# An edge-attention loop on one core: loads three steps ahead, edge terms before sums on TensorE, a weight matrix moved in halves

## The chip, the cores and the metric

The kernel runs on one core of a Trainium2 chip. The metric is the device time of one launch in microseconds (us). The engines that matter are TensorE (PE: matmuls; PEld is its loading of weights), VectorE (DVE), ScalarE (ACT), GpSimd (POOL) and SyncE (SP, which here only issues transfers). Each runs its own list of instructions in order, and they wait for one another through semaphores. A transfer (DMA) is issued from the queue of an engine and lands on its own.

## The reference

Four layers follow each other, each a graph network (gnn), a mixing step over all nodes (mix) and a feed-forward step (ffn), on 3,125 nodes of 256 features and 103,125 directed edges sorted by target. The change lies in layer 3's gnn:

```
feat_src = (feat @ W_n).reshape(N, 8, 32)
el = einsum('nhd,hdt->nht', feat_src, attn_l)     # t: 4 kinds of edge
er = einsum('nhd,hdt->nht', feat_src, attn_r)
em = einsum('ef,hft->eht', edge_attr_16, attn_m)
e  = einsum('eht,et->eh', el[src] + er[dst] + em, edge_attr_4) / 3.0
e  = where(e > 0, e, 0.2 * e)
a  = segment_softmax(e, dst)
rst = segment_sum(feat_src[src] * a[:, :, None], dst)

x = x + L3_gnn(layernorm(x)) + L3_mix(layernorm(x))
x = x + L3_ffn(layernorm(x))
```

(The three einsums over t are written as one here.) em is called the edge terms below. The kernel computes exp(e) unnormalised, sums exp(e) * z and exp(e) per target, and divides at the end.

## The kernel before, in words

The sorted edges lie in 806 columns of 128, one edge on each partition. `edge_attention` takes them in 101 steps of SC = 8 columns. The targets are cut into 25 tiles of 125 nodes; a step touches one or two of them (`here[i]`). Before the loop a table in device memory is written that holds for each source node its 8 x 33 values (32 features and a 1 for each head) and its 32 attention terms.

The parts of a step i, with engine and line:

- `load(i)`, SP: the targets of the step's 1,024 edges, copied to 125 partitions (`row`, two transfers through `part_dma`, L584 and L585, 4 buffers), the edge features (`ef`, L2584, 4 buffers) and a mask (`mask`, L2586, 5 buffers).
- `gather(i)`, POOL: eight indirect transfers (L2592), one for each column, bring the table's rows of the sources into `z_edge` (3 buffers).
- `targets(i)`, DVE: `hot` (L2605, 3 buffers) is 1 where an edge's target is node n of the tile.
- `products(i)`, PE: four matmuls of the edge features (L2617), and those of `hot` with the target terms `er` (L2620), both into the one buffer of `p_m`. ACT copies it to `m_sb` (L2622).
- `turn(i)`, PE: two transposes of `m_sb` into `p_e` (L2627), which puts an edge's terms on its own partition.
- `weights(i)`: DVE adds the source's terms and multiplies by the mask (`l`, L2635, L2638), sums and applies the leaky slope (`e`, L2640, L2641). ACT takes the exponential (`near_e`, L2643). DVE builds `oh`, the edges' one-hot targets (L2647), and multiplies `z_edge` by `near_e` (L2651).
- `sums(i)`, PE: for each column a matmul of `oh` with `z_edge` into the tile's accumulator `p_acc` (L2660, 2 buffers).
- `divide(i)`, DVE: where a tile is complete, the division and the addition to x (L2668 to L2672). After some tiles, work of the feed-forward step on them becomes available.

Between these, `piece()` is called twice a step. It advances other work by one yield: first layer 3's mixing step (`mix3`), then the transfers of the last weight matrix (`part3`, L2833, five transfers of 1 MB from SP, used only after the loop by the routed feed-forward step), and then the feed-forward's first half (`hidden3`).

The loop is written in a software pipeline. Turn i of it issues, in this order: `load(i+2)`, `sums(i-2)`, `gather(i+1)`, `products(i)`, `weights(i-1)`, a piece, `targets(i+1)`, `divide(i-2)`, `turn(i)`, a piece. PE and DVE keep exactly this order (`manual_schedule`). On ACT, POOL and SP a planner places the instructions by estimated times, so a change of the written order can change their order too.

Of the kernel before, what the change touches and what calls it, by code (L numbers as in the profile page):

```python
# [22 lines left out]
P = 128  # L23
# [3 lines left out]
C = 256  # L27
# [32 lines left out]
def dview(ap, offset, dims):  # L60
    return bass.AP(tensor=ap.tensor, offset=ap.offset + offset, ap=[list(d) for d in dims])
# [1560 lines left out]
class Dense(Net):  # L1622
# [903 lines left out]
    def edge_attention(self, x, xT, weights, pieces, then):  # L2526
# [10 lines left out]
        with ExitStack() as s:  # L2537
            with ExitStack() as s2:
# [4 lines left out]
                for t in range(NT):  # L2543
                    p = ps.tile([TP, C + 2 * EC], F32, name="p_z")
# [22 lines left out]
            def piece():  # L2567
                while work:
                    try:
                        return next(work[0])  # L2570
                    except StopIteration:
                        work.pop(0)
# [6 lines left out]
            def load(i):  # L2579
                c0, n = steps[i]  # L2580
                rows[i] = w.tile([TP, SC * P], I16, name="row", bufs=4)
                self.part_dma(nc.sync, rows[i], dview(dst_d, c0 * P, [[0, TP], [1, SC * P]]))
                efs[i] = w.tile([P, 2 * P], F32, name="ef", bufs=4)
                nc.sync.dma_start(efs[i], ins["edge16_s"][i])  # L2584
                masks[i] = w.tile([P, SC, 4], F32, name="mask", bufs=5)
                nc.sync.dma_start(masks[i][:, :n, :], ins["edge4_t"][:, c0:c0 + n, :])  # L2586

            def gather(i):
                c0, n = steps[i]
                zs[i] = wz.tile([P, SC, W], F32, name="z_edge")  # L2590
                for j in range(n):
                    nc.gpsimd.indirect_dma_start(  # L2592
                        out=zs[i][:, j, :], out_offset=None, in_=table,
                        in_offset=bass.IndirectOffsetOnAxis(ap=src[:, c0 + j:c0 + j + 1], axis=0))

            def strips(i, t):
                c0, n = steps[i]
                return max(cols[t][0] - c0, 0) // 2, min(-(-(cols[t][1] - c0) // 2), 4)

            def targets(i):  # L2600

                for t in here[i]:
                    q0, q1 = strips(i, t)
                    hots[i, t] = w.tile([TP, SC * P], F32, name="hot", bufs=3)
                    nc.vector.tensor_tensor(hots[i, t][:, q0 * 256:q1 * 256], rows[i][:, q0 * 256:q1 * 256],  # L2605
                                            node[:, t:t + 1].to_broadcast([TP, (q1 - q0) * 256]), OP.is_equal)

            def products(i):

                p_m = ps.tile([P, 2 * P], F32, name="p_m")  # L2610
                for t in [None] + here[i]:
                    for q in range(4):
                        qs = slice(q * 256, (q + 1) * 256)
                        s = slice(32 * q, 32 * q + 32)
                        last = ([None] + [u for u in here[i] if strips(i, u)[0] <= q < strips(i, u)[1]])[-1]
                        if t is None:
                            nc.tensor.matmul(p_m[s, :], attn_m[32 * q:32 * q + 16, :], efs[i][32 * q:32 * q + 16, :],  # L2617
                                             start=True, stop=(last is None))
                        elif strips(i, t)[0] <= q < strips(i, t)[1]:
                            nc.tensor.matmul(p_m[s, :], er[:, t, :], hots[i, t][:, qs], start=False, stop=(t == last))  # L2620
                terms[i] = w.tile([P, 2 * P], F32, name="m_sb")
                nc.scalar.activation(terms[i], p_m, AF.Copy)  # L2622

            def turn(i):
                p_e = ps.tile([P, 2, P], F32, name="p_e")
                for j in range(2):
                    nc.tensor.transpose(p_e[:, j, :], terms[i][:, j * P:(j + 1) * P], self.ident)  # L2627
                terms[i] = p_e

            def weights(i):  # L2630

                c0, n = steps[i]
                z = zs[i]
                l = w.tile([P, SC // 2, 2, EC], F32, name="l", bufs=1)
                nc.vector.tensor_add(l[:, :n // 2], terms[i].rearrange("p j (q f) -> p q j f", f=EC)[:, :n // 2],  # L2635
                                     z[:, :n, HW:].rearrange("p (q j) f -> p q j f", j=2))
                l4 = l.rearrange("p q j (t h) -> p (q j) t h", h=H)[:, :n]
                nc.vector.tensor_mul(l4, l4, masks[i][:, :n, :, None].to_broadcast([P, n, 4, H]))  # L2638
                e = w.tile([P, SC, H], F32, name="e")[:, :n, :]
                nc.vector.tensor_reduce(e, l4.rearrange("p c t h -> p c h t"), AX.X, OP.add)  # L2640
                nc.vector.scalar_tensor_tensor(e, e, 0.2, e, op0=OP.mult, op1=OP.max)  # L2641
                weight = near_e[:, i % 4, :n, :]
                nc.scalar.activation(weight, e, AF.Exp, scale=1.0 / 3.0)  # L2643
                for t in here[i]:
                    a, b = max(cols[t][0], c0), min(cols[t][1], c0 + n)
                    ohs[i, t] = w.tile([P, SC, TP], F32, name="oh", bufs=4)
                    nc.vector.scalar_tensor_tensor(ohs[i, t][:, :b - a, :], iota[:, None, :].to_broadcast([P, b - a, TP]),  # L2647
                                                   float(t * TP), dst[:, a:b][:, :, None].to_broadcast([P, b - a, TP]),
                                                   op0=OP.add, op1=OP.is_equal)
                zh = z[:, :n, :HW].rearrange("p c (h d) -> p c h d", h=H)  # L2650
                nc.vector.tensor_mul(zh, zh, weight[:, :, :, None].to_broadcast([P, n, H, D + 1]))  # L2651

            def sums(i):
                c0, n = steps[i]
                for t in here[i]:
                    a, b = max(cols[t][0], c0), min(cols[t][1], c0 + n)
                    if a == cols[t][0]:
                        acc[t] = ps3.tile([TP, HW], F32, name="p_acc")
                    for k in range(a, b):
                        nc.tensor.matmul(acc[t], ohs[i, t][:, k - a, :], zs[i][:, k - c0, :HW], start=(k == cols[t][0]), stop=(k == cols[t][1] - 1))  # L2660
# [16 lines left out]

            last = len(steps)
            with tc.manual_schedule(engines={mybir.EngineType.PE, mybir.EngineType.DVE}):
                for i in range(2):  # L2680
                    load(i)
                gather(0)
                targets(0)
                for i in range(last + 2):
                    if i + 2 < last:
                        load(i + 2)
                    if i >= 2:
                        sums(i - 2)
                    if i + 1 < last:
                        gather(i + 1)  # L2690
                    if i < last:
                        products(i)
                    if 1 <= i <= last:
                        weights(i - 1)
                    piece()
                    if i + 1 < last:
                        targets(i + 1)
                    if i >= 2:
                        divide(i - 2)
                    if i < last:  # L2700
                        turn(i)
                    piece()
                while work:
                    piece()
# [123 lines left out]
        turned = b[:, 2 * Q + 3 * C:2 * Q + 3 * C + KC * 3 * TP].rearrange("p (k n) -> p k n", k=KC)  # L2828
        return parts, norm, turned

    def part3(self, queue, out, f):

        queue.dma_start(out.rearrange("p (e c) -> p e c", c=C), self.ins["L3_ffn_Wd"][:, f * P:(f + 1) * P, :].rearrange("e p c -> p e c"))  # L2833

    def pieces3(self, w, ps, x, xn, xT, mix, parts):

        yield from self.mix3(w, ps, x, xn, xT, mix)
        for f, o in enumerate(parts):
            self.part3(self.nc.sync, o, f)
            yield  # L2840
            yield

    def hidden3(self, w, ps, x, room, t0, nt, weights, ones, hid_d):

# [557 lines left out]
```

## Time and profile before

| what | value |
|---|---|
| time, median of 3 runs | 5431.47 us (5419.27 to 5449.77) |
| the profiled execution | 5439.84 us |
| its span | 5438.0 us, 74,923 instructions |
| its mean granted TensorE clock | 0.924 |
| busy over the span | PE 87%, PEld 53%, DVE 62%, ACT 31%, POOL 28% |
| edge loop of layer 3 | about 3930 to 5230 us |
| clock granted in 3930 to 4430, 4430 to 5230 | 0.81, 0.86 |
| L2660 in the loop | 556.8 us of PE, 2,032 records, median 386 ns of one |
| L2651 in the loop | 236.5 us of DVE, 101, 2,342 ns each |
| L2592 | 769.7 us of POOL, 806, 955 ns each |
| table loads for L2643 on ACT | 35 of 1,283 ns |

The profile of one execution lists each instruction with its start and its duration. A line of the timeline gives the start in us from the span's start, the duration, engine, line, operation, output <- inputs, shapes, how many were joined, and in brackets how long the engine had been idle and what ended that. "issue" stands for a wait in which nothing was outstanding that the profile shows, "remote" for a releaser that the profile could not name. PE's matmuls are pipelined, so rows of PE overlap a little, and rows show when a matmul ran, not when another engine learned of it.

### The profile page before, as it was taken

The numbers are of one execution on the slowest core, as the hardware profiler recorded it, in microseconds if no ns is written. First come the engines' busy times: TensorE is split into PE (matmuls) and PEld (weight loads), VectorE is DVE, ScalarE is ACT, GpSimd is POOL, SyncE is SP. The second block draws the span as 40 slices with busy tenths as digits, with TensorE's granted clock in tenths as the row PEclk, the third lists the DMA queues.
The fourth block names the chain that finished last, engine by engine and source line by source line (L and its number), as shares of the span: only waits on it lengthen the run. The fifth ranks groups of instructions, "written<-read, shape, count | busy, mean of one in ns | idle before, by whom it ended". The sixth has DMA issues, their size and how long they took to land.

```text
span 5438.0 us, 74923 instructions
## 1 busy us (share of the span) xinstructions
PE 4737.5 (87%) x28141; PEld 2874.3 (53%) x28141; DVE 3392.9 (62%) x5768; ACT 1669.0 (31%) x2863; POOL 1514.4 (28%) x1413
## 2 busy tenths in 40 slices
PE   6789999889898999999989999999767767777778
PEld 4554434468465443785554335556445544444557
DVE  6878888755447988553359993223366655565643
ACT  2569878611431111102320103333211012222221
POOL 1108857534100000000010000000266555555623
PEclk8899999889999999999999999999888888888879
DMA  3885545511201111110001112000255545444535
GB/s 89 78 74 157 163 124 150 163 59 62 70 3 30 37 41 31 41 40 5 15 24 37 35 28 65 7 1 1 79 136 141 143 140 146 127 136 142 152 116 173
DMA packets 351061, 443.50 MB, mean 82 GB/s; under 512 B 144972, under 2 KB 270175, under 8 KB 350248
## 3 DMA queue, kind: packets, MB, share of 16 engines
q1 hardware_dynamic: 266710, 222.80, 17.8%
q0 software_dynamic: 55024, 175.53, 11.4%
q10 hardware_dynamic: 28959, 40.29, 2.4%
q8 instruction: 228, 3.74, 0.3%
q14 instruction: 140, 1.15, 0.1%
HBM read 384.87 MB, written 56.78 MB: 81 GB/s over the span
## 4 chain that ended last, share of the span: by engine, by line
PE 69%; DVE 9%; issue 6%; another core or an unknown queue 5%; ACT 4%; DMA 4%; POOL 2%; ACTq 0%; SPq 0%; DVEq 0%; POOLq 0%
PE acc L2316 9%; PE p_tr L751 8%; PE p_acc L2660 7%; PE p_n L2156 5%; PE acc L2448 5%; PE acc L2321 4%; PE p_h L751 4%; PE p_y L751 4%; PE p_q L751 4%; PE p_f L2201 3%; PE p_a L751 3%; DVE pt L2061 2%; PE p_t L751 2%; PE p_kvt L751 2%
## 5 line engine op out<-in xcount | busy, mean ns | idle before, releaser
L2061 DVE SCALAR_TENSOR_TENSOR pt<-q_head,bar,a 128x750 f32<-128x750 f32 (+4 forms) x975 | 889.1, 964 | 154.7 <-PE acc L2448 88.5
L2592 POOL DMA_INDIRECT z_edge<-tab,src_i x806 | 769.7, 955 | 557.3 <-PE p_acc L2660 223.5
L2316 PE MATMUL acc<-pt,zs 128*32 128x375 f32 (+1 forms) x6400 | 637.1, 497 | 23.3 <-DVE pt L2061 14.8
L2660 PE MATMUL p_acc<-z_edge,oh 128*125 128x264 f32 x2044 | 556.8, 435 | 41.1 <-DVE z_edge L2651 30.1
L2187 POOL TENSOR_TENSOR pt_far<-pt_far,a_far 128x1125 f32<-128x1125 f32 (+1 forms) x200 | 474.6, 2373 | 279.9 <-DMA a<-count_d 144.5
L2660 PEld LDWEIGHTS p_acc<-z_edge,oh 128*125 128x125 f32 x2044 | 435.4, 217 | 142.5 <-DVE z_edge L2651 33.4
L2142 DVE SCALAR_TENSOR_TENSOR pt<-q_here,bar,a 128x1000 f32<-128x1000 f32 (+1 forms) x384 | 456.0, 1250 | 46.2 <-DMA a<-count_d 21.0
L2156 PE MATMUL p_n<-pt,zs 128*64 128x500 f32 (+1 forms) x1600 | 405.1, 597 | 30.6 <-DVE pt L2142 30.2
L2316 PEld LDWEIGHTS acc<-pt,zs 128*32 128x32 f32 x6400 | 225.2, 110 | 347.3 <-issue 250.7
L2321 PE MATMUL acc<-pt,zs 128*32 128x375 f32 (+2 forms) x3200 | 352.9, 491 | 0.0
L1436 DVE SCALAR_TENSOR_TENSOR x<-p_y,sm,x 125x256 f32<-125x256 f32 x200 | 96.6, 483 | 380.6 <-PE p_y L751 380.6
L2651 DVE TENSOR_TENSOR z_edge<-z_edge,near_e 128x2112 f32<-128x2112 f32 (+1 forms) x101 | 236.5, 2342 | 136.7 <-ACT near_e L2643 101.3
L2627 PE MATMUL p_e<-ident,m_sb 128*128 128x128 f32 x202 | 52.4, 349 | 301.3 <-ACT m_sb L2622 187.5
L2448 PE MATMUL acc<-xn,pt 128*125 128x257 f32 (+1 forms) x1250 | 283.6, 382 | 10.6 <-DVE pt L2061 10.0
L2622 ACT ACTIVATE m_sb<-p_m 128x256 f32<-128x256 f32 x101 | 38.7, 383 | 727.2 <-remote 381.7
L2448 PEld LDWEIGHTS acc<-xn,pt 128*125 128x125 f32 (+1 forms) x1250 | 229.2, 187 | 56.9 <-DVE pt L2061 14.8
L2156 PEld LDWEIGHTS p_n<-pt,zs 128*64 128x64 f32 (+1 forms) x1600 | 156.8, 137 | 194.0 <-issue 106.2
L1420 ACT ACTIVATE h<-p_tr,bn 128x500 f32<-128x500 f32 (+1 forms) x224 | 161.4, 722 | 296.2 <-PE p_tr L751 296.2
L2201 PE MATMUL p_f<-pt_far,zs 128*64 128x375 f32 (+1 forms) x1200 | 245.0, 489 | 8.3 <-POOL pt_far L2187 8.3
L2185 ACT ACTIVATE pt_far<-q_log,log_s 128x1125 f32<-128x1125 f32 (+1 forms) x200 | 244.8, 1224 | 18.1 <-PE p_f L2201 15.6
L2186 ACT ACTIVATE pt_far<-pt_far,log_s 128x1125 f32<-128x1125 f32 (+1 forms) x200 | 247.0, 1235 | 6.5
L2605 DVE TENSOR_TENSOR hot<-row,near 125x1024 f32<-125x1024 int16 (+1 forms) x149 | 158.3, 1082 | 82.3 <-remote 69.0
(583 smaller groups left out, 7667.2 us busy)
## 6 DMA issues: line engine op xcount, KB each, us to landing
a<-count_d SPq DMA_DIRECT2D x384, 125.0 KB
a_far<-far_d SPq DMA_DIRECT2D x96, 281.2 KB
row<-dst_row SPq DMA_DIRECT2D x101, 224.0 KB
a<-count_d SPq DMA_DIRECT2D x144, 93.8 KB
ef<-in_edge_s SPq DMA_DIRECT2D x101, 128.0 KB
z_edge<-tab,src_i POOLq DMA_INDIRECT x806
count_d<-stage SPq DMA_DIRECT2D x12, 781.2 KB
q_head<-q_g ACTq DMA_DIRECT2D x24, 375.0 KB
```

The costliest lines, as they stand in the source:

```text
L751: self.nc.tensor.matmul(p, a, b, start=(i == 0), stop=(i == len(pairs) - 1))
L2061: self.nc.vector.scalar_tensor_tensor(pt[:K, :n], q, bar, a[:K, :n], op0=OP.max, op1=OP.mult)
L2142: nc.vector.scalar_tensor_tensor(pt[:K], q[:K], bar[:K, t, h:h + 1], a[:K].rearrange("p (j n) -> p j n", j=2), op0=OP.max, op1=OP.mult)
L2156: nc.tensor.matmul(accs[u][64 * j:64 * j + 64, :M * TP], zs[:K, t, h * W:h * W + 64], pt[:K, j, :], start=(t == 0), stop=(t == NS - 1))
L2186: nc.scalar.activation(f[:K], f[:K], AF.Exp, bias=log_s[:K, 1, t, h], scale=1.0 - 0.2)
L2187: nc.gpsimd.tensor_tensor(f[:K], f[:K], a[:K], OP.mult)
L2201: nc.tensor.matmul(far_accs[u][b][64 * i:64 * i + 64, :n], zs[:K, t, z:z + 64], fs[i][:K, b * n:(b + 1) * n], start=(t == 0), stop=(t == N ...
L2316: nc.tensor.matmul(acc[i // 2][r:r + 32, b, :b1 - b0], zs[:K, t, i * W + f:i * W + f + 32], pts[i][:K, b0:b1], **st)
L2321: nc.tensor.matmul(acc[2][32 * i:32 * i + 32, b, :b1 - b0], zs[:K, t, z:z + 32], pts[i][:K, b0:b1], **st)
L2448: nc.tensor.matmul(banks[i, j], pt[:K, j * TP:(j + 1) * TP], zs[:K, t, :], start=(t == 0), stop=(t == NS - 1))
L2592: nc.gpsimd.indirect_dma_start(out=zs[i][:, j, :], out_offset=None, in_=table, in_offset=bass.IndirectOffsetOnAxis(ap=src[:, c0 + j:c0 + j ...
L2660: nc.tensor.matmul(acc[t], ohs[i, t][:, k - a, :], zs[i][:, k - c0, :HW], start=(k == cols[t][0]), stop=(k == cols[t][1] - 1))
```

## The change

Three things are changed. Loads are issued for step i+3 instead of i+2 (three before the loop instead of two), with the same numbers of buffers. `products(i)` is issued first after the load, ahead of `sums(i-2)` and `gather(i+1)`. And each of the five parts of the last matrix is moved in two transfers of four experts (512 KB) with a yield after each, where it was one transfer with two yields; `part3` takes the range of experts for that, and the other caller, which gives none, gets all eight.

```diff
             with tc.manual_schedule(engines={mybir.EngineType.PE, mybir.EngineType.DVE}):
-                for i in range(2):
+                for i in range(3):
                     load(i)
                 gather(0)
                 targets(0)
                 for i in range(last + 2):
-                    if i + 2 < last:
-                        load(i + 2)
+                    if i + 3 < last:
+                        load(i + 3)
+                    if i < last:
+                        products(i)
                     if i >= 2:
                         sums(i - 2)
                     if i + 1 < last:
                         gather(i + 1)
-                    if i < last:
-                        products(i)
                     if 1 <= i <= last:
                         weights(i - 1)
                     piece()
...
-    def part3(self, queue, out, f):
-
-        queue.dma_start(out.rearrange("p (e c) -> p e c", c=C), self.ins["L3_ffn_Wd"][:, f * P:(f + 1) * P, :].rearrange("e p c -> p e c"))
+    def part3(self, queue, out, f, e0=0, e1=8):
+
+        queue.dma_start(out.rearrange("p (e c) -> p e c", c=C)[:, e0:e1, :],
+                        self.ins["L3_ffn_Wd"][e0:e1, f * P:(f + 1) * P, :].rearrange("e p c -> p e c"))
 
     def pieces3(self, w, ps, x, xn, xT, mix, parts):
 
         yield from self.mix3(w, ps, x, xn, xT, mix)
         for f, o in enumerate(parts):
-            self.part3(self.nc.sync, o, f)
-            yield
-            yield
+            for e in (0, 4):
+                self.part3(self.nc.sync, o, f, e, e + 4)
+                yield
```

## The prediction

> **What bounds the kernel now.** I read first the busy times by stretch, to separate the edge loop (3930 to 5230 us of the span) from the rest; no edit touches work outside it except the loads of L2833, whose results are used after 5233 us. Then the loop's list of waits (columns: engine, tile and line that wait, what released them, total us, times, longest), then the timeline of single steps, engine by engine.
>
> ```profile
> core 0: us, PE busy (x) PEld busy (x) DVE busy (x) ACT busy (x) POOL busy (x), PEclk, DMA share, GB/s
> 3930.00:5230.00 1300.00, 948.28 (x4991) 637.98 (x4992) 805.16 (x1171) 243.21 (x459) 749.11 (x788) 0.84 0.49 136
> ```
> ```profile
> ACT m_sb L2622 <- remote: 381.7, 31, 26.4
> POOL z_edge L2592 <- PE p_acc L2660: 223.5, 31, 16.4
> ...
> PE p_e L2627 <- ACT m_sb L2622: 187.5, 31, 24.1
> ```
> No engine is full: PE is busy 73%, POOL 58%, DVE 62%. The 101 steps run as a ring: z_edge has three buffers, so gather(i+1) needs sums(i-2); gathers feed the weights, these the multiplication L2651, that the sums. The starts of L2651 run from 3928.0 to 5225.1 us over 100 steps: 12.97 us a step.
>
> An undisturbed step:
> ```profile
> 4319.96 0.94 POOL L2592 DMA_INDIRECT z_edge<-tab,src_i  x1 [2.19 <-PE p_m L2620]
> ...
> 4331.87 0.94 POOL L2592 DMA_INDIRECT z_edge<-tab,src_i  x1 [2.21 <-PE p_m L2620]
> ```
> ```profile
> 4322.20 5.06 PE L2660 MATMUL p_acc<-z_edge,oh 128*125 128x264 f32 x22
> 4327.19 0.63 PE L2617 MATMUL p_m<-ef,attn_m 16*32 16x256 f32 x8
> 4327.76 0.62 PE L2620 MATMUL p_m<-hot,er 125*32 125x256 f32 x5
> ...
> 4330.72 0.38 PE L2620 MATMUL p_m<-hot,er 125*32 125x256 f32 x1 [0.34 <-issue]
> ```
> ```profile
> 4320.62 0.38 ACT L2622 ACTIVATE m_sb<-p_m 128x256 f32<-128x256 f32 x1 [3.73 <-PE p_h L1560]
> 4328.19 0.23 ACT L2643 ACTIVATE near_e<-e 128x64 f32<-128x64 f32 x1 [7.18 <-DVE l L2638]
> 4331.90 0.38 ACT L2622 ACTIVATE m_sb<-p_m 128x256 f32<-128x256 f32 x1 [3.48 <-PE p_m L2620]
> ```
> It lasts 11.91 us (4319.96 to 4331.87): 8 gathers of 0.94 at a distance of 1.25 (9.7 us in all), then 2.2 us until the next burst. The burst was released by sums that ended at 4327.2, and only with m_sb, 4.6 us later; the matmuls of L2620 after 4328 come 0.71 us apart, though an earlier group has 14 of them in 1.26 us. So while gathers run, other engines learn late that PE has finished, until about 1.7 us after the last gather. A disturbed step:
> ```profile
> 4520.53 0.63 PE L2617 MATMUL p_m<-ef,attn_m 16*32 16x256 f32 x8
> 4521.10 1.07 PE L2620 MATMUL p_m<-hot,er 125*32 125x256 f32 x16
> ...
> 4534.49 0.69 PE L2627 MATMUL p_e<-ident,m_sb 128*128 128x128 f32 x2 [11.86 <-ACT m_sb L2622]
> ```
> The products end at 4522.2, m_sb starts at 4534.06: two bursts had run back to back (4511.0 to 4530.8). Then everything was late at once, and the next burst stood 13.89 us. Of the 100 gaps between bursts 11 are of 8 us and more (140.3 us together), 15 under 1 us; the rest is mostly near 2.
>
> **The change part by part.**
>
> *Loads three steps ahead.* The same 101 loads; one more before the loop. Buffers stay at 4, 4 and 5, so row(i) waits for hot(i-4) and ef(i) for products(i-4) as before; SP's own waits in the loop name just these, L2584 <- PE p_m (190.4 + 148.1 us) and L584 <- DVE hot (128.1 us). Where a load runs into such a wait, program order was not its limit. Upper gain: what a consumer lost to a late load, 3.1 us (hot) and 10.4 us (m_sb), 13.5 in all, each one wait. Loss: four issues of 0.38 us, 1.5 us at the start if they lay on the path. What queues behind a waiting load on SP is Wd and the stores of hid_d; the longest of these SP waits is 13.4 us. I take 0.
>
> *Half-size Wd pieces.* Ten issues instead of five: 5 x 0.38 = 1.9 us more of SP time, the same bytes, and the same number of piece() turns (two a matrix). They were issued by 4344.6 and are needed after 5233: 888 us of cover. Without that cover it would cost the 1.9 us. Smaller transfers might disturb the neighbours less; the five lie in 335 of 1300 us, and the loop is as slow outside. 0.
>
> *Products ahead of sums.* No matmul is added. Three orders change, and gather(i+1) keeps its place right behind sums(i-2); POOL's queue holds nothing else that is moved past. On PE products(i) no longer stand behind sums(i-2): 5.5 us earlier (L2660: 556.8 us / 101). Sums(i-2), and with them the release of POOL, stand behind products(i), which wait for hot(i) on DVE. And ACT follows: in the built program m_sb(i+1) stands ahead of near_e(i) in 84 of 101 steps, against 14 now. What that costs can be seen where it happens now:
> ```profile
> 4165.78 0.38 ACT L2622 ACTIVATE m_sb<-p_m 128x256 f32<-128x256 f32 x1 [10.05 <-remote]
> 4166.06 0.22 ACT L2643 ACTIVATE near_e<-e 128x64 f32<-128x64 f32 x1
> ```
> The input of this near_e was there at 4159.66 (end of L2641); it waited 6.4 us behind m_sb, itself late for products that ended at 4161.5, and L2651 began at 4166.31 after 5.09 us of idle DVE. That becomes the rule. The ring is then: m_sb, near_e, z_edge (L2651), a piece of DVE work, hot (L2605, stands behind L2651 on DVE), next products, sums behind them, release of POOL. One turn:
> - PE to m_sb 0.10, m_sb 0.38, near_e 0.23, its table load 35 x 1.283 / 101 = 0.44: 1.15
> - handoff 0.03 (4166.28 to 4166.31), L2651 2.34, half of the pieces' DVE time 0.33 (some 65 us in 100 steps), hot 155.9 / 100 = 1.56, handoff 0.06: 4.32
> - products 1.82 (4159.71 to 4161.53); release of POOL 0.26 (PE 4544.43 to POOL 4544.69): 2.08
> - sums: 16 rows in 3.72 us at full clock, 22 in 7.95 after a pause of PE (4168.72), so for 20.2 matmuls 4.69 to 7.30; 5.51 is today's mean.
>
> Without the sums 7.55. The ends are 12.24 and 14.85 us a step. In the new ring 5.4 us lie between the start of m_sb and the next products (1.05 + 4.32); transposes (0.7) and pieces (237 us of rows / 100 = 2.4) fill some of it, so PE pauses 2.3 us in a mean step and up to 4.7 where no piece is at hand. Now it waits at the transposes for m_sb in 31 of 101 steps, 6 us each. I take 5.85 for the sums, a little above today's mean: the pauses come oftener and shorter. 7.55 + 5.85 = 13.40.
>
> The Trainium skill ("TensorE: Matmul & The Clock Gate", section "Why this matters for your kernels") speaks against this change: pauses of PE over some 3 us between bursts of matmuls should be avoided, or the clock falls to half. The granted clock of 0.84 in the loop and the 7.95 us group agree that it falls; by the rule taken strictly, the sums would cost the upper end in every step.
>
> I charge no wait for m_sb beyond the 0.10, though it may start early (products are issued 5.5 us sooner), and no stall of the kind of 4522; these are the rivals.
>
> **Sum.** 13.40 - 12.97 = +0.43 us x 100 steps = +43 us; the other parts 0. The profiled execution took 5439.8 us (span 5438.0 and 1.8 around it): 5483. The median of the runs is 5431.5, 8.4 lower: 5474.
>
> **The rivals.**
> - *A: the disturbed steps go.* Edge terms are asked of PE before the long sums, so m_sb(i) comes before the burst blinds it, and every step is like 4319.96. For it: the largest wait in the list is m_sb, and near_e's delay vanishes if m_sb is early. Against: hot(i) still follows L2651, and near_e now stands behind m_sb. 11 gaps fall from 140.3 to 11 x 2.1 = 23 us (-117), 15 short ones grow by 1.8 (+27): -90, 5341 us. Chance 0.22.
> - *B: no difference.* Sums keep 5.51: 13.06, +9 us, 5440; or a disturbed step less pays for it. For it: steps in which POOL sets the pace are 49 gaps of 1.7 to 2.6 us. Chance 0.22.
> - *C: PE at half clock.* The place is the pause between the transposes and the next products; it decides from the pause at which 20 sums cost 7.3. 14.85 - 12.97 = +1.88 a step, +188: 5620. Against: pieces of PE work lie in most pauses. Chance 0.10.
> - *That the loads don't do what they say*: buffers bind them in every one of these cases; it shifts no number.
>
> **How the numbers follow.** The forecast has 0.46, and its own range is 5445 to 5515 (13.1 to 13.8 a step). 0.5% is 27 us, about what a measurement here can tell from no change: 5404 to 5459. Faster is A, 0.22; no difference B, 0.22; slower the forecast and C, 0.56. The range of 5375 to 5560 takes in B, A up to a gain of 56 us (about half the long gaps gone), and C up to a loss of 129; it leaves out the full A and the full C.
>
> **What would show it.** Right: near_e directly behind m_sb on ACT; waits of L2617 or L2620 for hot on DVE, and of near_e's followers for m_sb; the 187.5 us of p_e waiting for m_sb mostly gone, since transposes come 5 us later than products; bursts released by p_acc in most steps with gaps of 3 us and more; the loop at 13.4 us a step and its clock at 0.84 or below; SP waiting for the same buffers. Wrong: gaps of 2.1 us throughout (A), the clock under 0.75 (C), hot waiting for row or Wd transfers in anybody's wait. The forecast fails first if the edge terms reach ACT well before the burst they now precede: then m_sb costs the ring nothing.

## The result and the profile after

| | before | after |
|---|---|---|
| median (6 runs each) | 5449.35 us | 5362.89 us |
| range | 5419.27 to 5453.88 | 5343.68 to 5366.40 |
| ratio, 95% interval | | 0.9853 [0.9834, 0.9872] |
| span of the profiled execution | 5438.0 | 5364.1 |
| L2651, first start to last start | 1297.0 | 1225.8 |
| gaps between bursts of gathers, sum of 100 | 341.7 | 265.4 |
| of these, 8 us and more | 11 (140.2) | 4 (45.1) |
| of these, under 1 us | 15 (4.6) | 17 (5.5) |
| m_sb(i) against the start of gather(i+1), median | 1.3 behind | 6.1 ahead |

The three runs of the first table are among the six of before. A gap is the time from the end of the eighth L2592 of a step to the start of the next step's first one, read from POOL's timeline. The kernel became 1.5% faster, where 0.8% slower was forecast. The loop gives 71 of the 74 us of span: 12.26 us a step instead of 12.97.

First the loop's stretch in the profile after (columns as in the same view of before), then its list of waits:

```profile
3930.00:5155.00 1225.00, 970.00 (x4975) 631.50 (x4976) 803.72 (x1169) 239.81 (x458) 754.58 (x788) 0.85 0.52 145
```
```profile
ACT m_sb L2622 <- PE p_acc L2660: 241.1, 44, 19.7
...
POOL z_edge L2592 <- PE p_acc L2660: 91.3, 21, 9.5
...
DVE z_edge L2651 <- ACT near_e L2643: 73.0, 24, 18.9
...
PE p_m L2620 <- DVE hot L2605: 69.9, 27, 13.9
...
PE p_e L2627 <- ACT m_sb L2622: 37.4, 8, 24.0
```

PE has nearly as many matmuls in a stretch that is 75 us shorter (4,975 against 4,991), and its granted clock is not lower (0.85, 0.84 before). PE's wait at the transposes for m_sb has gone from 187.5 to 37.4 us, POOL's for the sums from 223.5 to 91.3; a new wait of PE for hot (69.9 us, none before) takes up part of that. One step of the kernel after, all engines in one timeline:

```profile
4277.13 0.94 POOL L2592 DMA_INDIRECT z_edge<-tab,src_i  x1 [2.31 <-PE p_h L1560]
...
4278.91 1.22 PE L2620 MATMUL p_m<-hot,er 125*32 125x256 f32 x12 [0.74 <-DVE hot L2605]
...
4280.06 3.83 PE L2660 MATMUL p_acc<-z_edge,oh 128*125 128x264 f32 x16
...
4284.36 0.38 ACT L2622 ACTIVATE m_sb<-p_m 128x256 f32<-128x256 f32 x1 [14.45 <-PE p_h L1560]
4284.64 0.22 ACT L2643 ACTIVATE near_e<-e 128x64 f32<-128x64 f32 x1
...
4284.90 2.35 DVE L2651 TENSOR_TENSOR z_edge<-z_edge,near_e 128x2112 f32<-128x2112 f32 x1 [0.81 <-issue]
...
4289.10 0.95 POOL L2592 DMA_INDIRECT z_edge<-tab,src_i  x1 [2.25 <-PE p_m L2617]
```

The products end at 4280.1 and m_sb starts at 4284.4, still 4.2 us late, but in the middle of a burst (4277.1 to 4286.8). near_e goes right behind it and L2651 ends at 4287.2, before the next burst is released. In the disturbed step of before, m_sb came 11.9 us after the end of the products, and only then could the transposes and everything behind them go. Now the products run ahead of the long sums, and the sums stand between products and transposes as cover. Over the whole loop m_sb is hardly less late than it was: the time from the end of the last L2620 matmul to the start of m_sb, ACT being free, adds up to 287 us in 101 steps, against 334 before (worked out from the starts and ends in the traces). The lateness has been covered more than removed.

### The profile page after: what moved, and what is told of

It is laid out like the page before. It is cut to its first block, busy times and chain, and to the rows that moved or that the text cites. A ratio compares the mean times of both kernels' runs of the same rounds, so it can differ in the third digit from the quotient of the medians.

```text
span 5364.1 us, 74841 instructions
## 1 busy us (share of the span) xinstructions
PE 4754.3 (89%) x28141; PEld 2872.8 (54%) x28141; DVE 3393.5 (63%) x5768; ACT 1666.8 (31%) x2863; POOL 1519.9 (28%) x1413
## 4 chain that ended last, share of the span: by engine, by line
PE 70%; DVE 10%; issue 6%; DMA 4%; ACT 4%; another core or an unknown queue 3%; POOL 3%; ACTq 0%; SPq 0%; DVEq 0%; POOLq 0%
PE acc L2316 9%; PE p_tr L751 8%; PE p_acc L2660 7%; PE p_n L2156 5%; PE acc L2448 5%; PE p_h L751 4%; PE acc L2321 4%; PE p_y L751 4%; PE p_q L751 4%; PE p_a L751 3%; PE p_f L2201 3%; DVE pt L2061 2%; PE p_t L751 2%; PE p_kvt L751 2%
## 5 line engine op out<-in xcount | busy, mean ns | idle before, releaser
L2592 POOL DMA_INDIRECT z_edge<-tab,src_i x806 | 775.1, 962 | 481.0 <-issue 212.8
L2660 PE MATMUL p_acc<-z_edge,oh 128*125 128x264 f32 x2044 | 563.5, 435 | 27.1 <-issue 21.6
L2660 PEld LDWEIGHTS p_acc<-z_edge,oh 128*125 128x125 f32 x2044 | 425.4, 213 | 179.5 <-issue 87.0
L2651 DVE TENSOR_TENSOR z_edge<-z_edge,near_e 128x2112 f32<-128x2112 f32 (+1 forms) x101 | 236.8, 2345 | 168.9 <-issue 91.4
L2620 PE MATMUL p_m<-hot,er 125*32 125x256 f32 x1046 | 124.3, 482 | 127.4 <-DVE hot L2605 69.9
L2321 PEld LDWEIGHTS acc<-pt,zs 128*32 128x32 f32 (+1 forms) x3200 | 127.2, 109 | 153.4 <-issue 145.6
```

The lines of the kernel that those rows point to most:

```text
L2321: nc.tensor.matmul(acc[2][32 * i:32 * i + 32, b, :b1 - b0], zs[:K, t, z:z + 32], pts[i][:K, b0:b1], **st)
L2592: nc.gpsimd.indirect_dma_start(out=zs[i][:, j, :], out_offset=None, in_=table, in_offset=bass.IndirectOffsetOnAxis(ap=src[:, c0 + j:c0 + j ...
```

## The experiments

The kernel before did not take 5440 us in every experiment. Each group of runs was on one chip, each with runs of before beside it, and the groups are of two kinds: in two groups before took 5424 and 5435 us, as in the recorded pair (called late below), in four 5138 to 5157 (prompt). What tells them apart is the lateness of m_sb, as summed above: 334 us in the profile before and 318 in e17, but 7 to 10 us in all twelve profiles of the prompt groups. (The other profiles of the late kind have 269 to 329 us, and e9, in which bursts seldom follow each other at once, has 60.) The kernel before on a prompt chip (e6), in the same view:

```profile
4203.24 1.07 PE L2620 MATMUL p_m<-hot,er 125*32 125x256 f32 x12
...
4203.71 0.95 POOL L2592 DMA_INDIRECT z_edge<-tab,src_i  x1 [0.30 <-issue]
...
4204.45 0.38 ACT L2622 ACTIVATE m_sb<-p_m 128x256 f32<-128x256 f32 x1 [6.92 <-PE p_m L2620]
```

The products end at 4204.3 and m_sb starts at 4204.45, with gathers running on both sides of it. There POOL hardly stops: 89 of 100 gaps are under 1 us and the loop needs 10.4 us a step, near the 10.1 that eight gathers and a gap of 0.3 take.

| run | kernel | kind | us | before beside it | ratio, 95% interval |
|---|---|---|---|---|---|
| e1 | order alone | prompt | 5180.4 | 5144.5 | 1.0077 [1.0060, 1.0094] |
| e8 | order alone | prompt | 5192.4 | 5157.2 | 1.0067 [1.0049, 1.0084] |
| e12 | order alone | prompt | 5179.0 | 5145.2 | 1.0070 [1.0053, 1.0087] |
| e16 | order alone | late | 5348.1 | 5423.8 | 0.9863 [0.9831, 0.9896] |
| e2 | loads alone | prompt | 5143.9 | 5144.5 | 1.0004 [0.9995, 1.0014] |
| e13 | loads alone | prompt | 5141.7 | 5145.2 | 0.9999 [0.9989, 1.0008] |
| e17 | loads alone | late | 5424.7 | 5423.8 | 1.0000 [0.9983, 1.0016] |
| e3 | halves alone | prompt | 5147.9 | 5144.5 | 1.0007 [0.9997, 1.0016] |
| e4 | changed, copy written later | prompt | 5177.2 | 5144.5 | 1.0062 [1.0045, 1.0079] |
| e5 | the changed kernel | prompt | 5176.8 | 5137.8 | 1.0075 [1.0058, 1.0092] |
| e6 | the kernel before | prompt | 5146.8, one run | 5137.8 | |
| e7 | changed, hot early | prompt | 5155.4 | 5157.2 | 0.9997 [0.9987, 1.0007] |
| e18 | changed, hot early | late | 5338.5 | 5423.8 | 0.9834 [0.9799, 0.9870] |
| e9 | before and hop | late | 5461.1 | 5434.7 | 1.0049 [1.0031, 1.0066] |
| e10 | changed and hop | late | 5353.1 | 5434.7 | 0.9843 [0.9805, 0.9880] |
| e11 | hot early and hop | late | 5355.8 | 5434.7 | 0.9851 [0.9824, 0.9879] |
| e14 | before and hop | prompt | 5365.3 | 5145.2 | 1.0429 [1.0399, 1.0460] |
| e15 | changed and hop | prompt | 5175.6 | 5145.2 | 1.0056 [1.0038, 1.0073] |

**The three parts one by one.** e1 is the kernel before with the order alone:

```diff
-                    if i < last:
-                        products(i)
```
taken from behind `gather(i + 1)` and put ahead of `sums(i - 2)`.

> The kernel before with one part of the change alone: products(i) ahead of sums(i-2) and gather(i+1). Theory 1 (order: while gathers run, PE's ends are told to others late and one after the other, so whatever PE was given first is told first): the whole gain, 60 to 90 us below before (5362 +- 15), the loop's gaps of 8 us and more between bursts down from 11 to about 4, m_sb(i) about 6 us ahead of gather(i+1). Theory 2 (the loads three ahead do it, by taking late rows and features off the path): within 15 us of before. Theory 3 (both are needed): a gain of 20 to 50 us.

Slower by 0.8%: theory 1 fell as it was put, and 3 could not be told from a change of place. e2 is the loads alone:

```diff
-                    if i + 2 < last:
-                        load(i + 2)
+                    if i + 3 < last:
+                        load(i + 3)
```

> The kernel before with the loads three steps ahead alone. Theory 1: within 15 us of before, m_sb(i) 1.3 us behind the start of gather(i+1) as before. Theory 2: 60 to 90 us below before. Theory 3: 0 to 30 us below.

e3 is `part3` and `pieces3` of the change alone.

> The kernel before with the last matrix in half-size pieces alone. Theories 1, 2 and 3: within 15 us of before. If the 1 MB transfers held up rows, features or gathered rows: a gain, at most the lost time around 4009, 4108 and 4321 to 4345, some 20 us.

Neither moves the time. Since before was 5% faster here than in the recorded pair, the changed kernel and before were run again, unedited:

> The changed kernel itself, beside the kernel before, measured again: the kernel before took 5144 us beside the run of the order alone, and not 5431. Theory 1 (the order makes the gain, whatever else): cannot stand beside the run of the order alone, which came out 0.8% slower, unless this one is slower too, about 5180. Theory 3 (the order needs the loads three steps ahead): 5060 to 5100 where the kernel before takes 5144. Theory 6 (the sign hangs on the chip: on one that is 5% faster there are no long gaps that the order could take away): 0.5 to 0.9% slower where the kernel before takes about 5144, 1 to 2% faster where it takes about 5440.

> The kernel before, for its profile beside the last run. Theory 6: where the time is about 5144, the edge loop is some 1040 us long, not 1297, and has hardly a gap of 8 us between bursts of gathers (11 in the profile shown); where it is about 5440, the profile shown comes again.

Theory 6 held: 0.75% slower, as the order alone. On prompt chips the loop becomes 38 us longer (1036.9 to 1074.8) with no long gap to remove. The waits in e5:

```profile
ACT m_sb L2622 <- PE p_m L2620: 294.3, 69, 11.5
...
PE p_m L2620 <- DVE hot L2605: 141.7, 57, 7.7
```

The list of before on the same chip (e6) has no wait of PE's L2620 matmuls for hot (and 2.2 us on PEld). DVE's wait for near_e at L2651 hardly differs: 22.4 us in e5, 18.6 in e6.

**What the loss on prompt chips is.** e4 writes ACT's copy later, which was to put near_e(i) before m_sb(i+1) in all but 14 steps, as in the kernel before:

```diff
-                nc.scalar.activation(terms[i], p_m, AF.Copy)
+                terms[i] = p_m
...
             def turn(i):
+                m_sb = w.tile([P, 2 * P], F32, name="m_sb")
+                nc.scalar.activation(m_sb, terms[i], AF.Copy)
```

> The changed kernel with the copy of p_m to m_sb written in turn(i), after weights(i-1): ACT then has m_sb(i+1) ahead of near_e(i) in 14 of 101 steps, as before, and not in 84. PE and DVE keep the changed order. Theory 1: within 25 us of the changed kernel (near_e leaves a little earlier, m_sb a little later). Theory 4 (ACT's new order, m_sb first, is what makes the gain): back to 5420 to 5450. Theory 5 (my prediction's charge: near_e behind m_sb costs up to 6 us where it happens): 20 us and more below the changed kernel.

It takes 5177, as the changed kernel on another prompt chip. But the edit hardly does what it was to do: in the trace of e4 m_sb(i+1) still starts ahead of near_e(i) in 75 of 100 steps (84 in e5, 14 in e6). So e4 says little on ACT's order, and theories 4 and 5 stay open by it. e7 makes hot early:

```diff
+                    if i + 1 < last:
+                        targets(i + 1)
                     if 1 <= i <= last:
                         weights(i - 1)
                     piece()
-                    if i + 1 < last:
-                        targets(i + 1)
```

> The changed kernel with targets(i+1) written ahead of weights(i-1): DVE makes hot before it waits for near_e and multiplies z_edge, so that the products, which now stand first on PE, do not wait for L2651. Theory 7 (on a chip that tells PE's ends at once, the change costs what PE waits for hot, 187 us of waits at L2620 in the loop against next to none before): the loss of 38 us goes, within 10 us of the kernel before or below it; on a chip that tells them late, as in the recorded pair, 10 us and more below the changed kernel. Theory 8 (the loss is near_e behind m_sb, or the long sums behind the products): still 25 us and more above the kernel before on a chip that tells them at once.

> The order alone once more, for the chip it falls on. From the end of the last L2620 to m_sb, with ACT free, the recorded profile before has 334 us in 101 steps, the runs since 8. Theory 6 (the sign hangs on that lateness): where the sum is some 8 us, 0.6 to 0.9% slower than before; where it is some 300, 1.2 to 1.8% faster, as the recorded pair.

e7 is level with before while e8, the order alone on the same chip, is 0.67% behind; the wait of PE's L2620 for hot is gone from e7's list. The loss is hot standing behind the weights on DVE, L2651 the longest of them. The trace of e7 has m_sb(i+1) ahead of near_e(i) in 88 of 100 steps, so ACT's new order stands in a kernel that loses nothing. The kernel before with hot early was not run; there PE did not wait for hot, and so a gain from it is not expected, but not excluded by a run.

**Lateness put in by hand.** e9 and e14 (before), e10 and e15 (changed) and e11 (hot early) send m_sb through one more transfer, called the hop, and the transposes read the copy (both with one buffer):

```diff
-                terms[i] = w.tile([P, 2 * P], F32, name="m_sb")
-                nc.scalar.activation(terms[i], p_m, AF.Copy)
+                m_sb = w.tile([P, 2 * P], F32, name="m_sb", bufs=1)
+                nc.scalar.activation(m_sb, p_m, AF.Copy)
+                terms[i] = w.tile([P, 2 * P], F32, name="m_hop", bufs=1)
+                nc.scalar.dma_start(terms[i], m_sb)
```

> The kernel before with the edge terms made late on purpose: m_sb is moved by one more transfer (128 KB, from ACT's queue) into m_hop, which the transposes read; nothing else waits for it. It stands for the lateness of the recorded pair (334 us from the last L2620 to m_sb over 101 steps), at the one place where the transposes wait. Theory 1 (sums that stand between the products and the transposes cover a late m_sb; with nothing between, PE stands still): on a chip that tells PE's ends at once, PE waits at the transposes for the hop in nearly every step, about 2 to 2.5 us each; the kernel is 100 to 250 us slower than before. Theory 10 (the lateness of the sums' end for POOL, which this does not touch, made the long gaps): 0 to 40 us slower.

> The changed kernel with the same hop. Theory 1: the 5.5 us of sums cover the hop, 0 to 20 us over the changed kernel without it, so 20 us and more below the kernel before with the hop: the sign of the change turns round. Theory 10: as far above the changed kernel as the kernel before with the hop is above the kernel before, so still about 38 us behind it.

> The changed kernel with hot made early, with the same hop. Theory 1: the cover of the changed kernel without its loss: 0 to 20 us over the kernel before without a hop, and the fastest of the three. Theory 10: level with the kernel before with the hop.

These three runs fell on a late chip, where the lateness is there already. The hop then adds only 26 us to before, as theory 10 had it. e10 and e11 are level with each other and with the recorded pair (0.9843 and 0.9851 against 0.9853); the changed kernel without the hop was not run on this chip. In e9 the wait for the hop took the place of that for m_sb, and bursts hardly ran back to back any more (2 gaps under 1 us, 1 over 8); yet e9 is no faster for having lost the long gaps, since the others grew (364 us in all 100, 342 in the profile before). On a prompt chip the picture is clearer:

> The kernel before with the hop between m_sb and the transposes, for a chip of the prompt kind (on the late kind it was 26 us slower than before). Theory 1 (with nothing between products and transposes, PE stands still for a late m_sb): 100 to 250 us above before on the prompt kind. Theory 10 (only the late end of the sums, as POOL sees it, counts): 0 to 40 us above before.

> The changed kernel with the same hop, for a chip of the prompt kind. Theory 1: the sums cover the hop: 30 to 60 us above before, as without it (38), and so below the kernel before with the hop: the sign of the change turned round by one late transfer. Theory 10: level with it or above it.

Before and hop is 4.3% slower, changed and hop 0.6%, as without the hop: one late transfer turns the sign round, as theory 1 had it. What the hop makes is 44 gaps of 3 to 8 us (4 in e6) and only one of 8 us and more, so it imitates the late m_sb and not the long gaps of the late kind. PE's wait for the hop, first in e14, then in e15:

```profile
PE p_e L2629 <- DMA m_hop<-m_sb: 266.4, 82, 5.9
```
```profile
PE p_e L2629 <- DMA m_hop<-m_sb: 36.1, 17, 5.6
```

A step of e14 on PE shows what stands still and what follows:

```profile
4204.35 0.66 PE L2629 MATMUL p_e<-ident,m_hop 128*128 128x128 f32 x2 [4.81 <-DMA m_hop<-m_sb]
4204.80 7.85 PE L2662 MATMUL p_acc<-z_edge,oh 128*125 128x264 f32 x22
```

After 4.81 us of idle PE the 22 sums take 7.85 us, where 22 took 5.16 in e6. Over 3960 to 4900 us the granted clock is 0.84 in e14, 0.92 in e6 and 0.90 in e15.

**Order and loads on a late chip.**

> The order alone, a third time, for a chip of the late kind (kernel before near 5440 us; from the last L2620 to m_sb some 300 us in 101 steps). Theory 1 (there the order makes the whole gain): 60 to 95 us below before. Theory 3 (there the loads three ahead make it, or both are needed): within 25 us of before. On a chip of the prompt kind (before near 5145, 8 us): 35 us above before, as twice measured.

> The loads three ahead alone, for a chip of the late kind. Theory 1: within 25 us of before there (and within 15 on the prompt kind, as measured once). Theory 3: 30 us and more below before on the late kind.

These two fell on a prompt chip with e14 and repeat e1 and e2. The next three fell on a late one:

> The order alone, for a chip of the late kind (kernel before near 5440 us). Theory 1: there 60 to 95 us below before. Theory 3 (there the loads three ahead make the gain): within 25 us of before. On a chip of the prompt kind about 35 us above before, as three times measured.

> The loads three ahead alone, for a chip of the late kind. Theory 1: within 25 us of before. Theory 3: 30 us and more below before. On the prompt kind within 10 us of before, as twice measured.

> The changed kernel with hot made ahead of the weights, without the hop. On a chip of the late kind, theory 1: at the changed kernel's ratio to before or a little below it (0.975 to 0.987), since the order of PE is the same and the products no longer wait for L2651; so a version that gains there and loses nothing on the prompt kind. On the prompt kind level with before, as measured once.

The order alone gives 0.9863, which lies within the interval of the whole change; the loads alone give 1.0000 there. In e16 the gaps of 8 us and more are 2 (22.4 us), in e17 10 (120.9 us). PE's wait at the transposes went with them. First e17, from its page (matmuls, busy us, mean ns of one, then the idle time before them and what ended most of it), then e16, from its list of waits:

```profile
L2627 PE MATMUL p_e<-ident,m_sb 128*128 128x128 f32 x202 | 51.7, 345 | 286.8 <-ACT m_sb L2622 173.3
```
```profile
PE p_e L2627 <- ACT m_sb L2622: 13.2, 7, 7.8
```

POOL's wait for the sums fell too, from 209.9 to 91.7 us. No run separates the two on the late kind: that PE's wait at the transposes is what holds up the sums, and through them POOL, rests there on these lists and on e14 and e15. e18 is the best version overall: 1.7% faster than before on a late chip, level on a prompt one (e7). Its interval overlaps that of the changed kernel, so on late chips it isn't shown to be better than that.

## Why the prediction was wrong, point by point

- *What bounds the loop*: that PE's ends reach the others late while gathers run was read rightly from the profile before. m_sb is late in this way in the traces of the late kind and hardly at all on prompt chips, where the same change costs 38 us. That this lateness is what makes the late kind 5% slower is argued and not shown: the hop puts it in at one place only. That it differs from chip to chip could not be seen in one profile.
- *The step that failed* is the ring as it was added up, with its first term, "PE to m_sb 0.10", and the sentence "I charge no wait for m_sb beyond the 0.10, though it may start early". It lets m_sb follow the sums and the release of a burst, as before (1.3 us behind the burst's start), so the sums (5.85) and the release (0.26) stand in full between the products and m_sb. In the profile after m_sb(i) starts 6.1 us ahead of the next burst. From the end of the products to m_sb 3.5 us pass on average, where the sum has 6.21 (0.26 + 5.85 + 0.10); from m_sb to the end of the next products 9.0, where it has 7.19 (1.05 + 4.32 + 1.82). So the sums run beside the wait for m_sb and not ahead of it, and a step takes 12.26 us (12.4 from m_sb to m_sb), not 13.40. The text named an early m_sb as what would break it first; but that m_sb would then cost the ring nothing is not what happened, since 3.5 us of waiting are left (3.3 before).
- *Rival A* had the size, 90 us of gain against 86 measured, and only part of the reason; that its number is so near is in part luck. The long gaps went (11 of 140 us became 4 of 45: -95 against -117). The short ones did not grow by 27 us, they stayed (15 and 17), and those of 1 to 8 us grew by 18 (196.9 to 214.9). But m_sb does not come before the burst blinds it: in 69 of 101 steps it starts within a burst, and it is still late (287 us against 334), under the cover of the sums. Nor is every step like 4319.96: 54 gaps of 1.7 to 2.6 us, 49 before. That the order makes the gain, and takes most of the long gaps away, is shown by e16 against e17 on one chip.
- *near_e behind m_sb* was read rightly from the built program (the traces have it in 84 of 100 steps after, 14 before). A cost of it was not found, and it was not tested alone, since e4 does not take the order back. DVE's wait for near_e at L2651 went from 101.3 to 73.0 us in the recorded pair, but it is 105.6 in e16 with the new order and 72.2 in e17 with the old, so the order's share can't be told on late chips; on prompt ones it is 4 us in the whole loop (e5, e6).
- *Products behind hot behind L2651* is a true cost on prompt chips (e5, e7). On late chips e18 removes the wait, without a difference that can be told. That +43 was forecast and +38 measured on prompt chips is no confirmation: the forecast went from 12.97 to 13.40 us a step, there it goes from 10.37 to 10.75.
- *Sums and clock* (rival C): L2660 takes 563.5 us / 101 = 5.58 a step, not 5.85, at a clock of 0.85. The Trainium skill's rule against pauses of PE of more than some 3 us ("TensorE: Matmul & The Clock Gate", section "Why this matters for your kernels") agrees with e14, where PE pauses 3.2 us (266.4 / 82) at the transposes and the clock falls from 0.92 to 0.84; counted from the rows of the loop, e14 has 56 pauses of PE of 3 us and more (221 us), e6 12 (50 us). The changed order makes such pauses too on a prompt chip, 28 (127 us) in e5, at a clock of 0.90. On the late kind they were there already, 30 (257 us) before and 27 (139 us) after, and the clock did not fall further, so rival C did not come about.
- *Loads and halves at 0*: right. The loads alone are 1.0004, 0.9999 and 1.0000; the halves alone 1.0007 [0.9997, 1.0016]. The halves alone ran on a prompt chip only; on the late kind the order alone (0.9863) already gives the ratio of the whole change (0.9853) within the intervals, which reach 0.2 and 0.3% to each side. SP's list of waits before has more than the prediction took from it (200.9 us of L2584 <- remote, 105.8 us of L2586 <- DVE l, one wait of 63.2 us of L584 behind hid_d), which did not matter for the 0.

## What to carry to other kernels

Where an engine's results are read by another, put what the reader needs soonest first in the queue, and put independent work between producer and consumer on the same engine: 5.5 us of sums covered m_sb's lateness on late chips and a whole extra transfer on a prompt one. Then look at what the work that has been moved forward waits for itself, and move that along (hot, ahead of the weights), or the gain on one chip is a loss on another. And before forecasting from a ring of dependences, check for each link whether it follows the slowest engine's release or runs beside its work: here 6.2 us of sums and release were put in series where 3.5 us of waiting were measured.

## What the runs showed of the hardware that was not expected

The same kernel takes 5138 to 5157 us on four chips, and 5424 and 5435 on two others; in the recorded pair, whose chip is not on record, it takes 5449. Of the 293 us between the spans of the profile before and e6, 260 lie in this loop (1297.0 and 1036.9). On the late kind PE's increments of its semaphore, as the trace records them, come some 0.7 us or two or three times that apart while gathers run (4318.8, 4319.53, and 4320.6, 4321.31 in the profile before), and then in a row at 0.04 to 0.06 us around the gap between bursts (4319.53 to 4320.01); in e6 those of the sums come 0.45 us apart with gathers running. Some increments are missing from the record on the late kind: the profile before has 6,220 for 6,491 instructions that make one, e6 has 6,485, so the spacing is only as good as that. The matmuls' own durations differ little (L2660 has a median of 386 ns in both), but on the late kind PE itself also stands still between small matmuls without a releaser that the profile shows: 13.4 us in 30 waits at L2620 before, 35.9 in 28 after, none in e5 and e6. Why chips differ was not tried; each group of runs used one chip, so a property of the chip can't be told from one of the hour.
